# A graph network kernel on one Trainium2 core: the inverse square root of three layers' layer norms, by Newton's iteration on VectorE

## The chip, the cores and the metric

The kernel runs on one core of a Trainium2 chip. A core has a matrix engine (TensorE, in profiles PE), and three engines for the rest: VectorE (DVE), ScalarE (ACT) and GpSimd (POOL, almost unused here). A fifth, SyncE (SP), issues the transfers between the chip's memory and the on-chip memory. Each engine works through its own list of instructions in order and waits for others by semaphores, so an instruction that has to wait holds up everything behind it on its engine.

The metric is the time on the device, in microseconds (us). The kernel before takes 3764.35 us, the median of 3 runs (3759.23 to 3766.67).

## The reference

A batch of 16 graphs with 1024 nodes of 128 features passes through four layers, each a graph layer whose result is added to its input, and a layer norm over the features:

```python
def _layernorm(x, axis=-1, eps=1e-5):
    m = jnp.mean(x, axis=axis, keepdims=True)
    v = jnp.var(x, axis=axis, keepdims=True)
    return (x - m) / jnp.sqrt(v + eps)

x = _layernorm(x + L0(x, adj))   # sum over neighbours, times U, relu, over degree
x = _layernorm(x + L1(x, adj))   # masked attention: relu(q) relu(k)^T, softmax, times v
x = _layernorm(x + L2(x, adj))   # four-headed graph attention, weights from two vectors
x = _layernorm(x + L3(x, adj))   # neighbours thinned out row by row, three SAGE layers
```

Layer 1 needs q, k and v of the whole graph, and its result x2 is the input of layer 2. Layer 3 thins out the adjacency ("dilation", a sequential rule over rows) and has batch norms over all graphs between its three parts, so it can start only when all graphs are through.

## The kernel before

Nodes lie in 8 blocks of 128, one node per partition, features along the free axis. One function, `fuse`, does layers 0 to 2 and the dilation for all 16 graphs; `sage` does layer 3 after it.

In `fuse` the work is written as eleven generators, among them `layer0`, `layer1` (keys and values), `scores`, `values` (attention), `layer2` (weights and sides), `sides`, `layer2_sums`, `signs` (turns the loaded adjacency into the marks `has` and `over`), `widen` and `dilate`. Each yields a `Step` before the instructions that belong to it: the engine, a cost in us that the author estimates, and what it must follow. A planner, `Loom`, replays these costs: it always takes the step that can start first by its own reckoning, and among those of the same engine within 0.5 us the one that is due first. The due times come from a period of 160 us per graph and a phase and stretch for each generator. The instructions are written out in the order in which the planner takes the steps; the framework below it then still moves single instructions of one engine past others that don't depend on them. So a changed cost of one step can move any instruction of `fuse`.

The lines concerned:
- `Norm` is a layer norm of 8 blocks. `take` gathers statistics of a block (L547). `apply` combines them (L555 to L558 on VectorE), takes the square root on ScalarE (L560), then the reciprocal and the shift (L562 to L564 on VectorE), and applies both to the 8 blocks on ScalarE (L568). It runs three times for each graph, 48 times in all: for x1 after layer 0, for x2 after `values`, for x3 after layer 2.
- What follows x1: transposes on PE, the copy `xt` (L653), q and k (L681, L684). What follows x2: the copy `xt2` (also L653), a row of weights `t_row` (L818) that goes through memory and comes back spread (`row`, L763), and `st` (L835). What follows x3: its store to memory (L998).
- ScalarE has in the same stretches: `has` and `over` (L334, L337), `wide` (L352), the softmax `pr` (L719, an Exp), the copies `pt` (L737), the rows of the thinned adjacency `adt` (L531), the marks `sg` (L782), `ac` (L871, L872, Exp) and `bd` (L912, Exp).
- VectorE has: the running counts `up` and `ranked` (L367, L369) of the dilation, its rounds (`part`, L431 and L432; `thr`, L408 to L418; `ranked`, L494 to L505), the row minimum `low` (L716), `g` (L791, which needs `sg`), `sums` (L967) and the weights' `src` and `pieces` (L884 to L900).

[...]where the needed function is not in the table that is loaded, a table load (ACT_TABLE_LOAD in profiles) stands ahead of the instruction. The norms of layer 3 (L84, L1147 and the row norms at L1122) have square roots of their own, in `sage`.

Of the kernel before, what the change touches and what calls it, by code (L numbers as in the profile page):

```python
# [11 lines left out]
I32 = mybir.dt.int32  # L12
# [4 lines left out]
AF = mybir.ActivationFunctionType  # L17
ALU = mybir.AluOpType
PSUM = bass.MemoryType.PSUM
DRAM = bass.MemoryType.DRAM  # L20
P = 128
# [171 lines left out]
def fuse(S, ctx, a, x3, adt_d, viol, B=16):  # L193
# [18 lines left out]
    tc, nc = S.tc, S.nc  # L212
    const, ident, ones = S.scope(ctx, "fuse_const"), S.ident, S.ones
    V = nc.vector
    x_d, adj, mask = a["x"], a["adj"], a["nodemask"]
    a2 = a["L2_gnn_a"]
    H, DH = a2.shape[0], a2.shape[1] // 2
    N, TWOS, NEVER, ROUNDS = 8 * P, 2.0**24, 1e5, 2
    HI, NEG, REACH = 9e13, 9e15, 40.0
    D1, W3 = DH + 1, 3 * (DH + 1)  # L220

    two = ctx.enter_context(tc.tile_pool(name="fuse_two", bufs=2, space=PSUM))
    one = ctx.enter_context(tc.tile_pool(name="fuse_one", bufs=2, space=PSUM))
# [315 lines left out]
    class Norm:  # L539
# [8 lines left out]

        def apply(self, mark):

            yield Step("DVE", 0.4)
            t = sm.tile([P, 6, 8, 1], F32, name="ln_t")
            both, apart, var, sd, rs, nb = (t[:, i, :, :] for i in range(6))
            e, o, se, so = (self.st[:, :, i : i + 1] for i in (1, 4, 2, 5))
            V.tensor_tensor(apart, e, o, ALU.subtract)  # L555
            V.tensor_tensor(var, se, so, ALU.add)
            V.scalar_tensor_tensor(apart, apart, P / 4.0, apart, ALU.mult, ALU.mult)
            V.tensor_tensor(var, var, apart, ALU.add)  # L558
            yield Step("ACT", 1.5)
            nc.scalar.activation(sd, var, AF.Sqrt, bias=S.eps, scale=1.0 / P)  # L560
            yield Step("DVE", 0.35)
            V.tensor_tensor(both, e, o, ALU.add)  # L562
            V.reciprocal(rs, sd)
            V.scalar_tensor_tensor(nb, both, -0.5, rs, ALU.mult, ALU.mult)  # L564
            for q in range(2):
                yield Step("ACT", 1.55, mark=f"{mark} {q}")
                for c in range(4 * q, 4 * q + 4):
                    nc.scalar.activation(  # L568
                        self.y[:, c, :], self.y[:, c, :], AF.Identity, bias=nb[:, c, :], scale=rs[:, c, :]
                    )  # L570
# [667 lines left out]
def tile_gnn_stack(tc, a, out):  # L1238

    nc = tc.nc
    with ExitStack() as outer:
        flag = outer.enter_context(tc.tile_pool(name="flag", bufs=1))
        viol = flag.tile([P, 8], F32, name="viol")
        nc.vector.memset(viol, 0.0)
        with ExitStack() as ctx:
            S = Setup(ctx, tc)
            dram = ctx.enter_context(tc.tile_pool(name="fast_dram", bufs=1, space=DRAM))  # L1250
            x3 = dram.tile([16, 8 * P, P], F32, name="x3")
            adt_d = dram.tile([16, 8, P, 8 * P], F8, name="adt_d")
            with ExitStack() as first:
                fuse(S, first, a, x3, adt_d, viol)
            with ExitStack() as third:
                layers = [[a[f"L3_gnn_{n}{i}"] for n in ("Wr", "Wx", "b", "g", "be")] for i in (1, 2, 3)]
                sage(S, third, x3, a["nodemask"], adt_d, layers, a["L3_gnn_Wl"], a["L3_gnn_bl"], out)
            todo = flag.tile([1, 1], I32, name="todo")
            with tc.tile_pool(name="flag_ps", bufs=1, space=PSUM) as fp:
                ps = fp.tile([1, 8], F32, name="ps_flag")  # L1260
                nc.tensor.matmul(ps, S.ones[:, 0:1], viol, start=True, stop=True)
                total = flag.tile([1, 1], F32, name="total")
                nc.vector.tensor_reduce(total, ps, mybir.AxisListType.X, ALU.max)
                nc.vector.tensor_copy(todo, total)
        v = nc.values_load(todo[0:1, 0:1], min_val=0, max_val=16384)
        with tc.If(v > 0):
            general(tc, a, out)
# [676 lines left out]
```

## Time and profile before

| what | value |
|---|---|
| median of the runs | 3764.35 us (3759.23 to 3766.67) |
| profiled execution, its own time | 3761.21 us |
| its span, first to last instruction | 3759.5 us |
| mean granted clock of PE | 0.896 |
| PE busy | 3074.1 us (82%) |
| VectorE busy | 2937.3 us (78%), 7545 instructions |
| ScalarE busy | 2281.2 us (61%), 3889 instructions |
| table loads on ScalarE | 94, of 1283 ns each |

The profile is of one execution. A group line gives the source line, the engine and operation, what is written and read with shapes, and how often; then the busy time in all and the mean of one in ns; then the idle time of the engine just before these instructions and what ended it. A timeline line gives the start in us, the duration, the engine, the line, and in brackets the idle time before it. "The chain that ended last" follows the execution back from its end, at each step to what released it. `fuse` fills the first 2590 us or so.

### The profile page before, as it was taken

The numbers are of one execution on the slowest core, as the hardware profiler recorded it, in microseconds if no ns is written. First come the engines' busy times: TensorE is split into PE (matmuls) and PEld (weight loads), VectorE is DVE, ScalarE is ACT, GpSimd is POOL, SyncE is SP. The second block draws the span as 40 slices with busy tenths as digits, with TensorE's granted clock in tenths as the row PEclk, the third lists the DMA queues.
The fourth block names the chain that finished last, engine by engine and source line by source line (L and its number), as shares of the span: only waits on it lengthen the run. The fifth ranks groups of instructions, "written<-read, shape, count | busy, mean of one in ns | idle before, by whom it ended". The sixth has DMA issues, their size and how long they took to land.

```text
span 3759.5 us, 68072 instructions
## 1 busy us (share of the span) xinstructions
PE 3074.1 (82%) x26884; PEld 2402.0 (64%) x26884; DVE 2937.3 (78%) x7545; ACT 2281.2 (61%) x3889; POOL 2.3 (0%) x10
## 2 busy tenths in 40 slices
PE   5898878988889888898888989776699899899421
PEld 3777667776677767777667776655466666666321
DVE  3677878877888778887788777886588788888777
ACT  6678686786867868678686786753355344233100
POOL 0000000000000000000000000000000000000000
PEclk8898989999899998999989999888899999999655
DMA  4011111111111111111211111100433121112122
GB/s 118 29 61 58 53 63 39 53 59 61 63 38 54 57 63 58 39 57 55 65 58 40 57 52 63 51 29 25 95 101 90 47 68 57 57 57 73 43 73 63
DMA packets 223817, 220.11 MB, mean 59 GB/s; under 512 B 47808, under 2 KB 197824, under 8 KB 223488
## 3 DMA queue, kind: packets, MB, share of 16 engines
q1 hardware_dynamic: 223488, 215.67, 18.6%
q8 instruction: 213, 3.49, 0.4%
q14 instruction: 116, 0.95, 0.1%
HBM read 181.80 MB, written 33.82 MB: 57 GB/s over the span
## 4 chain that ended last, share of the span: by engine, by line
DVE 38%; PE 34%; ACT 18%; DMA 4%; issue 4%; SPq 1%; ACTq 0%; DVEq 0%
PE ps_s L708 6%; PE ps_g L1104 6%; DVE up L367 5%; PE ps_a L744 5%; ACT sg L782 5%; PE ps_z L1060 3%; PE ps_flip L574 3%; DVE t L1113 2%; ACT x L568 2%; DVE g L791 2%; DMA a<-in_adj_dram 2%; ACT has L334 2%; DVE ranked L369 2%; DVE both L390 2%; DVE ranked L494 1%
## 5 line engine op out<-in xcount | busy, mean ns | idle before, releaser
L782 ACT ACTIVATE sg<-row,st 128x1024 int8<-128x1024 f32 x512 | 555.6, 1141 | 7.3 <-DVE g L791 6.6
L1104 PE MATMUL ps_g<-pz,ad 128*128 128x384 bf16 (+1 forms) x3072 | 534.2, 327 | 2.2 <-DMA ad<-adt_d 2.2
L1104 PEld LDWEIGHTS <-ad 128*128 128x128 fp8e4 x3072 | 297.8, 98 | 199.8 <-DMA ad<-adt_d 12.1
L960 PE MATMUL ps_b<-pieces,g 128*128 128x198 bf16 x4096 | 372.6, 247 | 7.9 <-DVE sums L967 7.9
L960 PEld LDWEIGHTS <-g 128*128 128x128 fp8e4 x4096 | 351.8, 95 | 29.5 <-issue 28.8
L708 PE MATMUL ps_s<-kt,qt 128*128 128x512 f32 x512 | 315.5, 702 | 29.2 <-ACT pr L719 26.0
L935 PE MATMUL ps_m<-pieces,has 128*128 128x132 bf16 x3072 | 225.0, 241 | 127.5 <-ACT pieces L891 57.1
L935 PEld LDWEIGHTS <-has 128*128 128x128 fp8e4 x3072 | 218.5, 106 | 133.5 <-issue 133.4
L1121 ACT ACTIVATE sq<-xw 128x128 f32<-128x128 f32 x384 | 117.7, 307 | 306.1 <-DVE xw L1114 271.9
L744 PEld LDWEIGHTS ps_a<-vn,pt 128*128 128x128 f32 x2048 | 257.9, 199 | 61.9 <-ACT pt L737 30.5
L791 DVE TENSOR_TENSOR g<-sg,has 128x1024 int16<-128x1024 int16 x256 | 175.2, 685 | 153.0 <-ACT sg L782 151.7
L367 DVE TENSOR_TENSOR_SCAN up<-wide 128x1024 f16<-128x1024 bf16 x128 | 290.4, 2279 | 2.5 <-ACT wide L352 1.0
L744 PE MATMUL ps_a<-vn,pt 128*128 128x128 f32 x2048 | 270.5, 285 | 22.6 <-ACT pt L737 22.5
L719 ACT ACTIVATE pr<-ps_s,low 128x1024 f32<-128x1024 f32 x128 | 142.5, 1113 | 184.0 <-DVE low L716 179.8
L624 PE MATMUL ps_g<-py,has 128*128 128x128 bf16 (+1 forms) x3072 | 205.2, 224 | 34.6 <-DVE ranked L369 26.7
L716 DVE TENSOR_REDUCE low<-ps_s 128x1 f32<-128x1024 f32 x128 | 156.1, 1220 | 82.5 <-PE ps_s L712 82.4
L624 PEld LDWEIGHTS <-has 128*128 128x128 fp8e4 x3072 | 190.4, 100 | 37.8 <-DVE rdeg L631 20.9
L1113 DVE TENSOR_REDUCE t<-ps_g 128x128 f32<-128x384 f32 x384 | 206.3, 546 | 5.1 <-PE ps_g L1104 4.9
L531 ACT ACTIVATE adt<-ps_n 128x512 fp8e4<-128x512 f32 x256 | 146.2, 598 | 97.1 <-PE ps_n L521 88.8
L1060 PE MATMUL ps_z<-wzx,raw 128*128 128x256 f32 x768 | 191.9, 393 | 12.5 <-DVE xw L1068 5.6
L1224 PE MATMUL ps_y<-wl,raw 128*128 128x128 f32 x256 | 56.5, 410 | 161.7 <-DVE y L1228 161.7
L334 ACT ACTIVATE has<-a 128x1024 fp8e4<-128x1024 f32 x136 | 143.0, 1051 | 71.7 <-DMA a<-in_adj_dram 55.7
(239 smaller groups left out, 6574.2 us busy)
## 6 DMA issues: line engine op xcount, KB each, us to landing
a<-in_adj_dram SPq DMA_DIRECT2D x136, 512.0 KB
ad<-adt_d SPq DMA_DIRECT2D x384, 128.0 KB
row<-t_d SPq DMA_DIRECT2D x64, 512.0 KB
adt_d<-adt SPq DMA_DIRECT2D x128, 128.0 KB
xn<-x SPq DMA_DIRECT2D x32, 512.0 KB
x<-in_x_dram SPq DMA_DIRECT2D x16, 512.0 KB
x<-x SPq DMA_DIRECT2D x16, 512.0 KB
out_dram<-xn SPq DMA_DIRECT2D x16, 512.0 KB
```

Of the source, the lines that this page charges most:

```text
L334: nc.scalar.activation(has[c][:, r, :], t, AF.Sign, accum_out=num0[c][:, r : r + 1], saturate=False)
L367: V.tensor_tensor_scan(up, wide[k, r], wide[k, r], 0.0, ALU.add, ALU.max)
L624: nc.tensor.matmul(ps_g[:, k, 0:e], has[b][:, jb, ib * P : (ib + 1) * P], py[:, jb, q * P : q * P + e], start=(jb == 0 and q == 2), stop=( ...
L708: nc.tensor.matmul(ps_s[:, f : f + 512], qt[:, ib * P : (ib + 1) * P], kt[:, f : f + 512], start=True, stop=False,)
L744: nc.tensor.matmul(ps_a[:, 0:P], pt[:, c * P : (c + 1) * P], vn[:, c, :], start=(c == 0), stop=(c == 7))
L782: nc.scalar.activation(sg[:, k, :], rows[b, h], AF.Sign, bias=st[:, 1, h, ib : ib + 1], scale=-1.0)
L791: V.tensor_tensor(side[h, q // 2][:, q % 2 * 2 : q % 2 * 2 + 2, :].bitcast(I16), sg.bitcast(I16), has[b][:, 2 * q : 2 * q + 2, :].bitcast( ...
L935: nc.tensor.matmul(ps_m[:, u // 2, o : o + H * D1], has[b][:, ib, jb * P : (jb + 1) * P], pieces[:, ib, 1, :, t, :], start=(t == 0 and ib ...
L960: nc.tensor.matmul(ps_b[:, u // 2, (u % 2) * 2 * W3 : (u % 2 + 1) * 2 * W3], side[h, q][:, k, jb * P : (jb + 1) * P], pieces[:, 4 * q + k, ...
L1060: nc.tensor.matmul(ps_z[:, k, :], raw[:, b, c * P : (c + 1) * P], wzx, start=True, stop=True)
L1104: nc.tensor.matmul(ps_g[:, 0:width], adt[jb][:, ib * P : (ib + 1) * P], pz[:, jb, 0:width], start=(jb == 0), stop=(jb == 7),)
L1113: nc.vector.tensor_reduce(t, ps_g[:, 0 : 3 * P].rearrange("p (t d) -> p d t", t=3), AX.X, ALU.add)
```

## The change

The four instructions that combine the statistics stay. The square root on ScalarE and the reciprocal on VectorE go. In their place VectorE scales the variance and adds the epsilon, makes a first guess of 1/sqrt by arithmetic on the bits of the float read as an integer (minus half of them plus a constant), and improves it by three rounds of Newton's iteration, three instructions each. That makes one VectorE step of eleven more instructions less the reciprocal. The three steps (VectorE 0.4, ScalarE 1.5, VectorE 0.35) are one step of 1.6 on VectorE for the planner. All other steps and their costs, the 1.6 of `ac` among them, are as before.

```diff
-    D1, W3 = DH + 1, 3 * (DH + 1)
+    D1, W3, GUESS = DH + 1, 3 * (DH + 1), float(0x5F3759DF)
...
         def apply(self, mark):
 
-            yield Step("DVE", 0.4)
+            yield Step("DVE", 1.6)
             t = sm.tile([P, 6, 8, 1], F32, name="ln_t")
-            both, apart, var, sd, rs, nb = (t[:, i, :, :] for i in range(6))
+            both, apart, var, y, z, nb = (t[:, i, :, :] for i in range(6))
             e, o, se, so = (self.st[:, :, i : i + 1] for i in (1, 4, 2, 5))
             V.tensor_tensor(apart, e, o, ALU.subtract)
             V.tensor_tensor(var, se, so, ALU.add)
             V.scalar_tensor_tensor(apart, apart, P / 4.0, apart, ALU.mult, ALU.mult)
             V.tensor_tensor(var, var, apart, ALU.add)
-            yield Step("ACT", 1.5)
-            nc.scalar.activation(sd, var, AF.Sqrt, bias=S.eps, scale=1.0 / P)
-            yield Step("DVE", 0.35)
+            V.tensor_scalar(var, var, 1.0 / P, 1e-5, ALU.mult, ALU.add)
+
+            V.tensor_scalar(y.bitcast(I32), var.bitcast(I32), -0.5, GUESS, ALU.mult, ALU.add)
+            for _ in range(3):
+                V.tensor_tensor(z, y, y, ALU.mult)
+                V.scalar_tensor_tensor(z, z, -0.5, var, ALU.mult, ALU.mult)
+                V.scalar_tensor_tensor(y, z, 1.5, y, ALU.add, ALU.mult)
             V.tensor_tensor(both, e, o, ALU.add)
-            V.reciprocal(rs, sd)
-            V.scalar_tensor_tensor(nb, both, -0.5, rs, ALU.mult, ALU.mult)
+            V.scalar_tensor_tensor(nb, both, -0.5, y, ALU.mult, ALU.mult)
+            rs = y
             for q in range(2):
                 yield Step("ACT", 1.55, mark=f"{mark} {q}")
```

From L558 on, line numbers of the changed kernel are up to four higher: what was L568 is L572 there, and L567 is the last VectorE instruction of the norm (L564 before).

## The prediction

> **What bounds the kernel now.** I read the page first: busy times and the chain that ended last.
>
> ```profile
> PE 3074.1 (82%) x26884; PEld 2402.0 (64%) x26884; DVE 2937.3 (78%) x7545; ACT 2281.2 (61%) x3889; POOL 2.3 (0%) x10
> ...
> DVE 38%; PE 34%; ACT 18%; DMA 4%; issue 4%; SPq 1%; ACTq 0%; DVEq 0%
> ```
>
> No engine is full, and the chain hops between three. So a microsecond saved on ScalarE (ACT) is worth something only where ScalarE paces. Next, the groups of ScalarE that the norms cause:
>
> ```profile
> L560 ACT ACT_TABLE_LOAD x47 | 60.3, 1283 | 0.8
> ...
> L719 ACT ACT_TABLE_LOAD x29 | 37.2, 1283 | 0.5
> ...
> L871 ACT ACT_TABLE_LOAD x16 | 20.5, 1283 | 0.3
> ...
> L560 ACT ACTIVATE ln_t<-ln_t,eps 128x8 f32<-128x8 f32 x48 | 14.4, 300 | 121.1 <-DVE ln_t L558 120.7
> ```
>
> Each square root brings a table load, and the next Exp (L719, L871) brings another. Where do they lie? The page's slices show layers 0 to 2 until about 2590 us; between the x2 norms of two batches the chain repeats every 157.05 us (1070.16 to 1227.21). I cut one such period, from 1227.2, into 16 windows; the columns are window, length, busy us (instructions) of PE, weight loads, DVE, ACT and POOL, granted clock, DMA share, GB/s:
>
> ```profile
> 1237.01:1246.83 9.81, 9.63 (x119) 8.29 (x117) 1.32 (x4) 6.88 (x12) 0.00 (x0) 1.00 0.47 162
> 1246.83:1256.64 9.81, 7.57 (x125) 7.16 (x123) 8.64 (x14) 9.26 (x13) 0.00 (x0) 1.00 0.08 28
> 1256.64:1266.45 9.81, 2.48 (x35) 2.02 (x33) 9.81 (x23) 8.12 (x10) 0.00 (x0) 0.74 0.10 40
> ...
> 1305.70:1315.51 9.81, 9.81 (x83) 8.13 (x82) 6.83 (x12) 9.34 (x15) 0.00 (x0) 1.00 0.48 159
> 1315.51:1325.33 9.81, 6.54 (x68) 3.46 (x67) 8.80 (x26) 7.94 (x13) 0.00 (x0) 0.70 0.40 130
> 1325.33:1335.14 9.81, 7.45 (x51) 5.40 (x49) 6.86 (x29) 8.57 (x15) 0.00 (x0) 0.50 0.11 41
> ...
> 1374.39:1384.20 9.81, 9.20 (x97) 6.76 (x95) 9.29 (x33) 0.81 (x3) 0.00 (x0) 1.00 0.18 53
> ```
>
> From 1256.6 to 1276.3 VectorE (DVE) is 100% busy, and near the x2 norm (last row) 95%; in the second row it shares the load with ScalarE. From 1305.7 to 1335.1, the start of a batch's attention, ScalarE is busy 9.34 + 7.94 + 8.57 = 25.9 of 29.4 us, while PE has holes and its clock falls to 0.50: there ScalarE paces. The timeline of that stretch:
>
> ```profile
> 1317.79 1.28 ACT L719 ACT_TABLE_LOAD   x1
> 1319.08 1.11 ACT L719 ACTIVATE pr<-ps_s,low 128x1024 f32<-128x1024 f32 x1
> ...
> 1325.97 1.28 ACT L560 ACT_TABLE_LOAD   x1
> 1327.27 0.30 ACT L560 ACTIVATE ln_t<-ln_t,eps 128x8 f32<-128x8 f32 x1
> ...
> 1333.92 1.28 ACT L719 ACT_TABLE_LOAD   x1
> ```
>
> Three table loads and a root stand in it (those of the x3 norm). The first is on the chain itself (one period earlier, at 1160.68).
>
> **What the Trainium skill says.** "ScalarE: Activation LUTs", section "Table sets: the hidden batching unit": exp and sqrt are in different sets, so alternating them loads every time. The trace agrees: 47 loads at the root, 46 at an Exp. The same page, "What ACT_TABLE_LOAD costs", gives 1283 ns plus a drain of 1380 ns. The trace shows the 1283 ns, but pr starts at 1319.08, 0.01 us after the load ended at 1319.07: no drain, so I use 1.283 us. "VectorE: DVE Perf Modes", section "The DRAIN you can't avoid": a read of what the instruction before wrote needs a semaphore. The built program has such a wait on each dependent link. "TensorE: Matmul & The Clock Gate", section "What's actually happening": PE falls to half clock after an idle window of about 3.4 us. The windows agree (0.50, 0.70).
>
> **The change part by part.** All is per steady batch unless said.
>
> *Removed table loads.* In the built program's order 94 loads stand ahead of the end before, and two after (the first Sign; layer 3's first root). 92 × 1.283 = 118.0 us, and 48 roots of 0.30 = 14.4: ScalarE loses 132.4 us, 8.3 per batch. What is it worth?
> - In 1305.7 to 1335.1: 3 × 1.28 + 0.3 less the 0.09 that neighbours overlap = 4.1 us. At least the 1.28 on the chain counts. Not all: `has` waits for the adjacency load twice here (1.11 and 1.21 us), and these waits grow when the rest gets quicker; the release-to-landing time is about 3.5 us (over ends 1312.86, has starts 1316.14). I take 3.0, bounds 1.3 and 4.1.
> - The x1 root (1279.02): ScalarE's L568 started 0.1 us after it was free, but VectorE was full and gave the L564 it needs no earlier (1126.00 one period before, so 1283.05; L568 started at 1283.28). Worth 0; covered by VectorE, and 1.6 if that cover were gone.
> - The x2 root: L568 waited 2.19 us for VectorE's L564; worth 0. Without that cover it would be 1.6.
> - L871's load (1254.79) lies before VectorE's full stretch, hidden by scans; 0, bound 1.3.
>
> *Added VectorE work.* Per norm, eleven instructions come and one (reciprocal, 195 ns) goes: +10, in all +480. None is in the trace, but the same shapes are (128x8, 160 to 167 ns). Independent ones start 0.08 us apart (61.72, 61.81, 61.90), a dependent one 0.19 us after its source (L557 61.98, L558 62.17). The new chain has 13 dependent links. In the new order a steady cycle spans two batches, six norms; between the first and last instruction of each stand 18, 14, 18, 1, 17 and 15 other VectorE instructions. So five norms are interleaved and cost 10 × 0.08 = 0.8 us; the sixth, an x2, is exposed: 4 × 0.08 + 13 × 0.19 = 2.8, less the 0.6 that its seven old ones took interleaved, about 2.0 to 2.2. By place: x1 (VectorE full) +0.8; x2 (95% full) mean of 0.8 and 2.0, +1.4; x3 (VectorE at 70 to 90%, something idle) +0.3, bounds 0 and 0.8. Sum +2.5. Behind the later L572 (old L568) on ScalarE's queue stand adt, the copy xt2 and with them t_row; these prices include their delay.
>
> *Moved instructions.* The planner orders by its own costs (a VectorE step of 1.6 now, no ScalarE step of 1.5), so everything moves. I looked for what matters. Before, after x2's apply, ScalarE runs three `sg` before the first `wide`, and VectorE's first `g` stands ahead of `ranked`: it waits 5.98 us for sg (at 1245.79) with scans behind it. This is the hole in the first window row (DVE 1.32 of 9.81). In the new order no sg stands before the wides, and the first g comes after five or more scans. 3 × 1.04 = 3.1 us less stands before wide; adt's waits for PE remain, so I take 2.0 (0 to 3.1). The queue of SP: the eight loads of an adjacency now all stand ahead of the x3 store, before six did; the last two were released at 1342 anyway. Worth 0.
>
> *Sum.* −3.0 − 2.0 + 2.5 = −2.5 per batch. About 14 batch periods are steady: −35 us. Layer 3's first root now loads its table: +1.3, hidden or not. 3761.2 (the profiled execution) − 34 = 3727; the median of the runs lies 3.1 above that execution, so about **3731**.
>
> **The rivals.**
> *Slower: VectorE sets the pace.* Place: 1256.6 to 1276.3 and 1374.4 to 1384.2. If the moved wides gain nothing and the attention start gives only its 1.3, then with x3 at 0.8 the batch gets −1.3 + 0.8 + 1.4 + 0.8 = +1.7; 14 × 1.7 = 24, about 3789. The two-batch cycle speaks for it: from one x2 norm to the next the new order has 361 and 307 VectorE entries in turn (a run of one instruction counted once), where before it was 303 each time. If the heavy batch is paced by VectorE, its 27 above the mean, at 127 us / 334 = 0.38, are 10 us, of which the light one may return only half: 5 per pair, 2.5 a batch, 35 in all, 3799. It decides once ScalarE's relief in the attention start and the wides' gain together fall below the 2.5 that VectorE pays. Against: DVE is only at 70 to 90% there.
> *No change.* The relief turns into waits of L572 for L567 and of `has` for the load: ScalarE idles more by what it saved. The gain of 2.5 is met by 2.5: 3764.
> *The change doesn't do it* (another function still needs a second table): excluded, the built order has the two loads only.
>
> **How the numbers follow.** This kernel can be told from no change at about 0.2%, 7.5 us. Faster, near 3731: 0.53. No change: 0.09. Slower, 3789 to 3799: 0.38, high because a replanned order can lose several us per batch in places I didn't cost. Range: best per batch −4.1 − 3.1 + 2.2 = −5 gives 3694; above, the VectorE rival at 3789 with little more: 3692 to 3800. The likeliest case alone: 3700 to 3752.
>
> **What would show it.** Two table loads; ScalarE near 2149 us busy, VectorE up by about 40 to 50; no 6 us wait of g for sg after x2; the stretch from the first has to the second pt about 3 us shorter, PE's clock there above 0.5; the pair of batches near 309 us instead of 314. Wrong if L572's waits for L567 pass 5 us a batch, if `has` waits for loads grow by 2 us or more, or if the pair takes over 314.

## The result, and the profile after

The changed kernel takes **3857.45 us** (median of 4 runs, 3851.76 to 3866.49). The kernel before, run beside it, takes 3763.93 us. The ratio is 1.0252 (95% interval 1.0239 to 1.0265): the change costs about 94 us, 2.5%. The forecast was 3731, and 3800 was the end of its range.

The first part of the page after, and its chain that ended last:

```profile
PE 3102.7 (81%) x26868; PEld 2431.7 (63%) x26884; DVE 2993.8 (78%) x8025; ACT 2157.8 (56%) x3749; POOL 2.3 (0%) x10
...
PE 41%; DVE 39%; ACT 11%; DMA 5%; issue 2%; SPq 1%; ACTq 0%; DVEq 0%
```

The sizes of the parts came close to the forecast: ScalarE lost 123.4 us of busy time (132.4 were expected), VectorE gained 56.5 us (40 to 50) and 480 instructions. ScalarE's share of the chain fell from 18% to 11%, but PE's rose from 34% to 41%. ScalarE's groups of table loads in all:

```profile
L334 ACT ACT_TABLE_LOAD x1 | 1.3, 1283 | 0.8 <-PEq L1934 0.8
L1126 ACT ACT_TABLE_LOAD x1 | 1.3, 1283 | 0.0
```

The 92 loads are gone; the change did what it says. So the time went elsewhere. The last scaling of a norm starts at 2673.6 us (L572), against 2585.4 before (L568): `fuse` ends 88 us later. In the steady part the order repeats every two batches, and two batches are one window here, first of the kernel before, then of the changed one (window, length, busy us and instructions of PE, weight loads, VectorE, ScalarE, GpSimd; granted clock, DMA share, GB/s):

```profile
1227.20:1541.30 314.10, 272.57 (x2712) 221.69 (x2711) 253.66 (x625) 239.36 (x348) 0.00 (x0) 0.92 0.17 55
```

```profile
1449.20:1777.00 327.80, 275.56 (x2719) 223.66 (x2720) 261.81 (x687) 223.37 (x331) 0.00 (x0) 0.89 0.16 53
```

The pair takes 13.7 us more. ScalarE does 16.0 us less in it. VectorE does 8.2 us more and idles 5.6 us more as well (327.80 - 261.81 = 66.0 against 314.10 - 253.66 = 60.4). Over the whole kernel the span grows by 90.3 us; 56.5 of that is VectorE's busy time and 33.8 its idle time (span less busy time). Where is the idle time? The list of waits (who waited for whom: us in total, times, longest), before:

```profile
DVE g L791 <- ACT sg L782: 151.7, 91, 6.0
...
DVE ranked L369 <- PE ps_n L521: 37.1, 15, 9.9
```

and after:

```profile
DVE ranked L369 <- PE ps_n L521: 176.6, 15, 14.7
...
PE ps_flip L578 <- ACT x L572: 107.2, 17, 12.1
...
DVE g L795 <- ACT sg L786: 84.8, 58, 4.6
```

The wait of `g` for `sg` shrank by 67 us, as the prediction said. In its place `ranked` waits 140 us longer for PE. `ranked` has one buffer. PE's `stays` (L515 to L521) read the thinned rows of one dilation out of it, and the next dilation can't write its first row before they are done. But these 140 us are not all new. VectorE's timeline in the kernel before, from the last drop of one dilation (L505) to the first row of the next (start, duration, line; in brackets the idle time before):

```profile
1229.23 0.67 DVE L505 TENSOR_TENSOR ranked<-x,y 128x1024 bf16<-128x1024 bf16 x1
...
1230.03 4.46 DVE L367 TENSOR_TENSOR_SCAN up<-wide 128x1024 f16<-128x1024 bf16 x2
...
1239.11 0.23 DVE L835 COPY st<-ps_st 128x64 f32<-128x64 f32 x1 [3.59 <-PE ps_st L828]
...
1245.79 0.69 DVE L791 TENSOR_TENSOR g<-sg,has 128x1024 int16<-128x1024 int16 x1 [5.98 <-ACT sg L782]
1247.82 1.29 DVE L369 TENSOR_TENSOR ranked<-up,wide 128x1024 f16<-128x1024 f16 x2 [1.34 <-PE ps_n L521]
```

`st`, `g` and `ranked` share one hole here, and `ranked` closes it: no third scan stands in it, since `wide` has two buffers and `ranked` gives them back. The same stretch in the changed kernel, around an x2 norm:

```profile
1584.32 2.28 DVE L367 TENSOR_TENSOR_SCAN up<-wide 128x1024 f16<-128x1024 bf16 x1
1586.52 0.66 DVE L505 TENSOR_TENSOR ranked<-x,y 128x1024 bf16<-128x1024 bf16 x1
...
1587.44 2.28 DVE L367 TENSOR_TENSOR_SCAN up<-wide 128x1024 f16<-128x1024 bf16 x1
...
1589.94 0.17 DVE L555 TENSOR_TENSOR ln_t<-ln_st 128x8 f32<-128x8 f32 x1
...
1592.81 0.17 DVE L567 SCALAR_TENSOR_TENSOR ln_t<-ln_t 128x8 f32<-128x8 f32 x1
...
1608.51 1.29 DVE L369 TENSOR_TENSOR ranked<-up,wide 128x1024 f16<-128x1024 f16 x2 [14.42 <-PE ps_n L521]
```

and PE's, in the same stretch:

```profile
1593.56 0.33 PE L578 MATMUL ps_flip<-ident,x 128*128 128x128 f32 x1 [2.85 <-ACT x L572]
```

Two scans of the next dilation stand ahead of the x2 norm; the norm (3.0 us, its links 0.20 us apart) runs after the last drop (L505); PE's transposes of x2 wait for its scaling, and the rest of the stays stands behind them on PE's queue. Then VectorE idles 14.42 us, in one wait where there were three. Before, the norm began 7.5 us ahead of the end of the last drop in every steady batch, so it ran among the drops. After, it begins 7.6 us ahead in one batch and 2.8 us behind in the next.

The late norm does hold up the stays, but the sum changes little. From the end of the last drop to the first row of the next dilation it is 17.9 us in a steady batch before, and about 21.3 (norm behind) and 16.3 us (norm ahead) in turn after: 0.9 more in the mean. VectorE's idle time in these 15 stretches, added up from the timelines, is 170.9 us before and 182.1 after. So only 11 of the 34 us of added idle time lie in this hole. `ranked` waits for 9.1 us there even where the norm is ahead; most of the 140 us have only changed their name.

### The profile page after: what moved, and what is told of

Its sections match the earlier page's. It is cut to its first block, busy times and chain, and to the rows that moved or that the text cites. A ratio compares the mean times of both kernels' runs of the same rounds, so it can differ in the third digit from the quotient of the medians.

```text
span 3849.8 us, 68421 instructions
## 1 busy us (share of the span) xinstructions
PE 3102.7 (81%) x26868; PEld 2431.7 (63%) x26884; DVE 2993.8 (78%) x8025; ACT 2157.8 (56%) x3749; POOL 2.3 (0%) x10
## 4 chain that ended last, share of the span: by engine, by line
PE 41%; DVE 39%; ACT 11%; DMA 5%; issue 2%; SPq 1%; ACTq 0%; DVEq 0%
PE ps_g L1108 7%; DVE up L367 5%; PE ps_s L712 5%; PE ps_a L748 4%; PE ps_m L939 4%; PE ps_z L1064 3%; ACT sg L786 3%; PE ps_b L964 3%; PE ps_flip L578 3%; PE ps_g L628 2%; DMA a<-in_adj_dram 2%; DVE t L1117 2%; DVE both L461 2%; DVE g L795 2%; ACT has L334 1%
## 5 line engine op out<-in xcount | busy, mean ns | idle before, releaser
L964 PEld LDWEIGHTS <-g 128*128 128x128 fp8e4 x4096 | 350.0, 96 | 21.3 <-issue 20.5
L939 PEld LDWEIGHTS <-has 128*128 128x128 fp8e4 x3072 | 220.3, 107 | 100.2 <-issue 98.9
L723 ACT ACTIVATE pr<-ps_s,low 128x1024 f32<-128x1024 f32 x128 | 142.0, 1109 | 219.5 <-DVE low L720 166.6
L748 PE MATMUL ps_a<-vn,pt 128*128 128x128 f32 x2048 | 261.0, 280 | 1.8 <-ACT pt L741 1.4
L795 DVE TENSOR_TENSOR g<-sg,has 128x1024 int16<-128x1024 int16 x256 | 175.1, 687 | 96.3 <-ACT sg L786 84.8
L628 PE MATMUL ps_g<-py,has 128*128 128x128 bf16 (+1 forms) x3072 | 240.6, 234 | 9.9 <-ACT has L334 5.6
L628 PEld LDWEIGHTS <-has 128*128 128x128 fp8e4 x3072 | 214.7, 106 | 16.6 <-ACT has L334 6.2
L369 DVE TENSOR_TENSOR ranked<-up,wide 128x1024 f16<-128x1024 f16 x128 | 85.9, 682 | 176.6 <-PE ps_n L521 176.6
L741 ACT COPY pt<-ps_flip 128x1024 f32<-128x1024 f32 x128 | 129.0, 1009 | 105.7 <-PE ps_flip L578 104.3
```

The lines of the kernel that those rows point to most:

```text
L628: nc.tensor.matmul(ps_g[:, k, 0:e], has[b][:, jb, ib * P : (ib + 1) * P], py[:, jb, q * P : q * P + e], start=(jb == 0 and q == 2), stop=( ...
L748: nc.tensor.matmul(ps_a[:, 0:P], pt[:, c * P : (c + 1) * P], vn[:, c, :], start=(c == 0), stop=(c == 7))
L795: V.tensor_tensor(side[h, q // 2][:, q % 2 * 2 : q % 2 * 2 + 2, :].bitcast(I16), sg.bitcast(I16), has[b][:, 2 * q : 2 * q + 2, :].bitcast( ...
L939: nc.tensor.matmul(ps_m[:, u // 2, o : o + H * D1], has[b][:, ib, jb * P : (jb + 1) * P], pieces[:, ib, 1, :, t, :], start=(t == 0 and ib ...
L964: nc.tensor.matmul(ps_b[:, u // 2, (u % 2) * 2 * W3 : (u % 2 + 1) * 2 * W3], side[h, q][:, k, jb * P : (jb + 1) * P], pieces[:, 4 * q + k, ...
```

## The experiments

Two theories stood first. **Work**: VectorE's added instructions cost the time, in any order. **Order**: the planner's new order costs it, whatever the arithmetic. All times are medians, beside the kernel before on the same chip (3759 to 3765 us).

### The two halves, each alone

The first kernel has Newton's iteration with the old planned steps, so that the order is nearly that of before:

```diff
-            yield Step("DVE", 1.6)
+            yield Step("DVE", 0.4)
...
+            yield Step("ACT", 1.5)
+            yield Step("DVE", 0.35)
             V.tensor_scalar(var, var, 1.0 / P, 1e-5, ALU.mult, ALU.add)
```

> Newton's iteration as in the changed kernel, but the planner is told the old three steps (VectorE 0.4, ScalarE 1.5, VectorE 0.35), so the order of all other work is nearly that of before. Theory 'order' (the 94 us come from the order that the planner made of the new costs): the arithmetic alone gives what the prediction's first two steps gave, -3.0 + 2.5 = -0.5 a batch, so 3740 to 3775, and the pair of batches takes about 313 us. Theory 'work' (VectorE's 50 us more are the cause in any order): 3820 to 3860, the pair about 325.

Measured: 3810.52 us, ratio 1.0126 (1.0109 to 1.0143), so +46 us, between the two expectations.

The second has the old arithmetic with the new planned step (one of 1.6 on VectorE, with the root inside it):

```diff
-            yield Step("DVE", 0.4)
+            yield Step("DVE", 1.6)
...
-            yield Step("ACT", 1.5)
             nc.scalar.activation(sd, var, AF.Sqrt, bias=S.eps, scale=1.0 / P)
-            yield Step("DVE", 0.35)
```

> The arithmetic of before (the root on ScalarE, 94 table loads back), with the changed kernel's planner costs (one VectorE step of 1.6 that also holds the root), so the order is nearly that of after. Theory 'order': as slow as the changed kernel or slower, 3850 to 3900, the pair 328 to 332 us. Theory 'work': near before, 3755 to 3785, the pair about 314.

Measured: 3812.99 us, ratio 1.0134 (1.0117 to 1.0151), so +49 us. Neither theory alone holds: the halves are 46 and 49, and together (95) they make the whole 94. The wait of `ranked` for `ps_n` is 157.9 us in the second kernel and 83.6 in the first, so it comes mostly with the order. But the loop through `ranked` is not what makes the second kernel slow: from the last drop to the next first row it takes about 18.2 and 14 us in turn, less than the 17.9 before, and still the kernel is 49 us slower. (VectorE also waits 10.2 us there for the root inside its step, 6.7 more than before, which the order's 49 include; and this order brings 80 table loads, not 94.)

### The price of the loads, and of the iteration

The third kernel leaves the square root out, so its norms divide by the variance plus epsilon; the table loads go with it, and the planned order stays:

```diff
-            nc.scalar.activation(sd, var, AF.Sqrt, bias=S.eps, scale=1.0 / P)
+            nc.scalar.activation(sd, var, AF.Identity, bias=S.eps, scale=1.0 / P)
```

> The order and steps of before, with Identity in place of Sqrt: the square root of the norms of layers 0 to 2 is left out (they divide by the variance plus epsilon), and with it the table loads. It prices the removal of the loads alone, the prediction's first step: -3.0 a batch (1.3 to 4.1) would be 3707 to 3746, about 3722. If the relief turns into other waits (theory 'hidden'): 3755 to 3765. Theories 'order' and 'work' both allow either.

Measured: 3752.15 us, ratio 0.9966 (0.9952 to 0.9979): the loads were worth 12 us, 0.75 a batch, under the prediction's lowest bound of 1.3 and a little more than "hidden" has. Newton in the old order therefore costs 3810.5 - 3752.2 = 58 us, 3.6 a batch. Where did the rest of the relief go? ScalarE's timeline at the start of a batch's attention, in the kernel before:

```profile
1319.08 1.11 ACT L719 ACTIVATE pr<-ps_s,low 128x1024 f32<-128x1024 f32 x1
...
1335.22 1.11 ACT L719 ACTIVATE pr<-ps_s,low 128x1024 f32<-128x1024 f32 x1
...
1338.45 1.11 ACT L719 ACTIVATE pr<-ps_s,low 128x1024 f32<-128x1024 f32 x1 [1.52 <-DVE low L716]
```

and without the root:

```profile
1312.34 1.11 ACT L719 ACTIVATE pr<-ps_s,low 128x1024 f32<-128x1024 f32 x1
...
1324.64 1.10 ACT L719 ACTIVATE pr<-ps_s,low 128x1024 f32<-128x1024 f32 x1
...
1332.42 1.11 ACT L719 ACTIVATE pr<-ps_s,low 128x1024 f32<-128x1024 f32 x1 [6.07 <-DVE low L716]
```

The second softmax row comes 12.3 us after the first instead of 16.1, but the third comes 20.1 after it instead of 19.4: the relief has turned into a wait of 6.07 us. It is the same over the whole kernel: ScalarE's waits of `pr` for `low` grew from 179.8 to 252.0 us and those of L560 for L558 from 120.7 to 166.6, together by 118 us, as much as the loads took. Behind the third row's wait is PE, which runs at a granted clock of 0.56 there before and 0.58 without the root (windows from the first to the third row). PE's first transposes of the attention wait for VectorE's count in both kernels, in the kernel before and then without the root:

```profile
1327.84 1.94 PE L574 MATMUL ps_flip<-ident,pr 128*128 128x128 f32 x8 [1.03 <-DVE gone L452]
```

```profile
1321.47 1.94 PE L574 MATMUL ps_flip<-ident,pr 128*128 128x128 f32 x8 [1.03 <-DVE gone L452]
```

From the first `pt` to the row minimum of the third row it is 7.3 us before (1329.81 to 1337.14) and 7.4 without the root (1323.74 to 1331.10): that is mostly PE's matmuls at half clock (the eight transposes above take 1.94 us, and 1.07 at 1339.01, at full clock). The Trainium skill, "TensorE: Matmul & The Clock Gate", section "What's actually happening", has PE fall to half clock after an idle window of about 3.4 us. The traces agree in kind, over stretches a little shorter than that: the granted clock falls from 1.00 to 0.50 after 2.9 us in which PE worked 0.6 us (before), and after 2.6 us with 0.2 us of work (without the root). ScalarE was the busiest engine there, and yet not the one that set the pace.

The fourth kernel has six rounds of the iteration for three, in the old order:

```diff
-            for _ in range(3):
+            for _ in range(6):
```

> As the first kernel (Newton, old steps), with six rounds of the iteration for three: nine more VectorE instructions a norm, 27 a batch. Theory 'order': what VectorE's small instructions cost is 0.08 us each where other work is interleaved and 0.19 each where not, so 0.7 to 1.7 us a norm and 2.2 to 5.1 a batch at most, half of it hidden: 15 to 50 us above the first kernel. Theory 'work': VectorE paces, so at least the 50 us that the first three rounds cost again and more, 70 to 100 us above the first kernel.

Measured: 3902.86 us, ratio 1.0379 (1.0362 to 1.0396), 92 us above three rounds. That is 92.3 / (48 x 9) = 0.214 us for each added instruction, a little over the 0.20 us between dependent links, though "half of it" hidden was expected under the order theory. That it is so near the 0.20 is partly chance: VectorE's busy time grew by 44 us and its idle time by 45, and its wait of `st` for PE, which follows the x2 norm by way of the scaling and the transposes, from 104.6 to 166.4.

The fifth, again with the old steps, runs the iteration on GpSimd, which does nothing else:

```diff
+            G = nc.gpsimd
...
             for _ in range(3):
-                V.tensor_tensor(z, y, y, ALU.mult)
-                V.scalar_tensor_tensor(z, z, -0.5, var, ALU.mult, ALU.mult)
-                V.scalar_tensor_tensor(y, z, 1.5, y, ALU.add, ALU.mult)
+                G.tensor_tensor(z, y, y, ALU.mult)
+                G.tensor_tensor(z, z, var, ALU.mult)
+                G.tensor_scalar(z, z, -0.5, 1.5, ALU.mult, ALU.add)
+                G.tensor_tensor(y, y, z, ALU.mult)
+            yield Step("DVE", 0.35)
             V.tensor_tensor(both, e, o, ALU.add)
             V.scalar_tensor_tensor(nb, both, -0.5, y, ALU.mult, ALU.mult)
```

> Old steps and order; the iteration runs on GpSimd, which is idle otherwise (14 small instructions a norm there, since it takes a round in four), so VectorE loses the reciprocal and gains nothing, and the table loads stay away. Theory 'occupancy' (what Newton cost in the old order, 58 us above the version without root, is VectorE's time): 3740 to 3765. Theory 'latency' (it is the length of the chain that the norm's scaling waits for): longer than on VectorE, since GpSimd takes at least as long for each link: 3810 or above, to 3880.

Measured: 3862.20 us, ratio 1.0255 (1.0238 to 1.0272). The result falls to the latency theory by its number, but the list of waits shows that it doesn't separate the two:

```profile
DVE ln_t L570 <- POOL ln_t L567: 114.7, 45, 4.0
```

The last instruction of the norm stayed on VectorE, and VectorE stood still for it 114.7 us: a chain of some 3.9 us did not fit into the room that the order leaves. Against the kernel without root this one is 110 us slower. Leaving out the waits for something else behind them, the instructions of the 48 norms hold VectorE for 34 us without the root, 78 with Newton and 134 with six rounds (from the starts in the timeline): 44 more for 58 us of run time, then 56 more for 92. Beside that, VectorE's idle time from the last drop to the next first row, which the x2 norm leads up to, grows from 168 to 193 and 225 us. In the GpSimd kernel the hold stays at 34 us, and the 114.7 us of waiting come back as 110. So both count in the old order: the time that a norm takes of VectorE, and the waiting behind a norm that ends later. These runs don't part the two any further.

### Is it the two-batch order?

The prediction's rival had uneven batches as its ground. Three kernels keep the changed text and differ only in the planned cost, 1.3 here, 0.75 and 0.4 in the others:

```diff
-            yield Step("DVE", 1.6)
+            yield Step("DVE", 1.3)
```

> The changed kernel with a planned cost of 1.3 for the norm's one VectorE step in place of 1.6; all else is the same text. In the built order every batch has the same number of VectorE instructions (325 between two x2 norms; in the changed kernel 363 and 286 in turn). Theory 'two-batch' (the order's 49 us come from uneven batches): near the kernel with Newton and the old steps, 3795 to 3820, one batch near 160.5 us. Theory 'one step' (any order that sees the norm as one VectorE step, with no room for ScalarE in it, loses): 3845 to 3870.

> The same with a planned cost of 0.75, the sum of the two VectorE steps of before; 321 VectorE instructions in every batch. Theory 'two-batch': 3790 to 3820. Theory 'one step': 3845 to 3870.

> The same with a planned cost of 0.4. Here the built order alternates again, with 302 and 343 VectorE instructions in turn, about half the unevenness of the changed kernel (286 and 363). Theory 'two-batch': between the even orders and the changed kernel, 3820 to 3850. Theory 'one step': 3845 to 3870. If it lies with the even ones, the count of instructions by batch is not what matters.

Measured: 3873.17 (1.0282; 1.0265 to 1.0299), 3863.09 (1.0263; 1.0246 to 1.0280) and 3844.12 us (1.0211; 1.0194 to 1.0228). The last lies where "two-batch" had it, but the two even orders are no faster than the changed kernel, and an uneven one is: unevenness isn't the cause. For the "one step" theory, a kernel with three steps again, the empty one told as 2.0. Against the changed kernel:

```diff
-            yield Step("DVE", 1.6)
+            yield Step("DVE", 0.4)
...
                 V.scalar_tensor_tensor(y, z, 1.5, y, ALU.add, ALU.mult)
+            yield Step("ACT", 2.0)
+            yield Step("DVE", 0.35)
             V.tensor_tensor(both, e, o, ALU.add)
```

This edit differs in two things from the Newton kernel with the old steps, not in one as the expectation has it: the empty step is 2.0 and not 1.5, and the iteration stands ahead of it, in the first step, where that kernel has it in the third.

> Newton with three planned steps as before, only that the empty ScalarE step is told as 2.0 in place of 1.5; every batch has 324 VectorE instructions. Theory 'three steps' (an order that leaves room between the norm's steps keeps the old time): 3800 to 3820, as with 1.5. Theory 'tuned point' (the old costs happen to give a good order, and any other planned cost loses some 1%): 3830 to 3875.

Measured: 3894.04 us, ratio 1.0349 (1.0332 to 1.0367), 84 us above the kernel with 1.5. So three steps alone don't make an order fast, and the "one step" theory doesn't hold as it was put; which of the two differences costs the 84 us was not tested. It is the third theory, "tuned point", that stands here by its direction; its range ended at 3875.

### Taking away the wait for the buffer

The rows of `ranked` come from ten buffers for eight, so that two rows of the next dilation needn't wait for PE; for the room, `xt0` shares the buffers of `d` and `y`:

```diff
-        ranked[c] = p1.tile([P, 8, N], F16, name="ranked")
+        ranked[c] = [p1.tile([P, N], F16, name="ranked", bufs=10) for _ in range(8)]
...
-                xt = p2.tile([P, 4, P], F32, name="xt0")
+                xt = p4.tile([P, 4, P], F32, name="xt0", tag="t2k", bufs=2)
```

It was tried on the changed kernel, on the kernel before, and on Newton with the old steps.

> The changed kernel, with the eight rows of ranked (the tile that the next dilation must get back from PE's stays) taken from ten row buffers in place of eight, so that two rows of the next dilation can be written before PE has read the last drop; for the room, xt0 shares the buffers of d and y. Theory 'dilation loop' (what the new order lost is the 12 us wait of ranked L369 for PE's ps_n, 176.6 us against 37.1 before): two scans and two ranked rows, 5.8 us, run in each of 15 waits, so the wait falls to about 90 and the time by 50 to 85 us, to 3770 to 3810. Theory 'symptom' (VectorE is behind for another reason and would only wait elsewhere): 3845 to 3860, the wait moves to row 2 or to another line.

> The kernel before with the same ten row buffers. Its wait of ranked for ps_n is 37.1 us in all. Theory 'dilation loop': all of it can go, 3730 to 3750. Theory 'symptom': 3758 to 3768.

> Newton with the old steps (3810.5 measured) and ten row buffers; its wait of ranked for ps_n is 83.6 us. Theory 'dilation loop': 5.8 us in each of 15 waits at most, 3735 to 3770. Theory 'symptom': 3800 to 3812.

Measured: 3779.55 us (1.0038; 1.0026 to 1.0051), **3728.39 us** (0.9905; 0.9888 to 0.9921) and 3763.48 us (0.9996; 0.9987 to 1.0005). They gain 78, 36 and 47 us. The second is faster than both kernels of this case, 1.0% faster than the one before. In all three, two rows of the next dilation are now written ahead of the wait, and VectorE idles less from the last drop to the first row that has to wait: by 86, 62 and 76 us. In the changed kernel the wait fell from 176.6 to

```profile
DVE ranked L369 <- PE ps_n L521: 92.6, 15, 9.2
```

as the "dilation loop" theory has it. In the third it did not fall (83.6 and 84.9 us); the wait of `st` for PE went there, from 104.6 to 0.9. The loop through this buffer is thus a limit of all three kernels, the one before too, and only what is left of the difference tells of the change: with ten rows it costs 51 us (3779.6 against 3728.4), with eight 94. With ten rows the two orders with Newton differ by 16 us only (3779.6 and 3763.5), against 47 with eight. The edit also gives every row a buffer of its own and moves `xt0`; a kernel with eight such rows, which would part these from the two added rows, was not run.

Does that hold without Newton, and does the loop also hide ScalarE's relief? Two kernels with ten rows tell: the one without root (the square root is left out again), and the old arithmetic in the changed order. Their edits are those above, combined.

> The order of before, ten row buffers for ranked, and Identity for Sqrt: the square root of these norms is left out, and with it the table loads. Against the kernel before with ten row buffers (3728.4). Theory 'hidden by the loop' (the ranked buffer's loop hid ScalarE's relief): the relief grows to 25 us or more, 3690 to 3703. Theory 'ScalarE is not the limit anywhere for long': 8 to 16 us as with eight rows, 3712 to 3720.

> The root and table loads of before in the changed kernel's order, with ten row buffers. With eight it took 3813.0, 49 us more than before, and its wait of ranked for ps_n was 157.9 us. Theory 'all in that wait': 5.8 us in each of 15 waits come back, 3725 to 3745, as fast as the kernel before with ten rows. Theory 'half of it': 3750 to 3775, as the pair with Newton (3763.5 in the old order, 3779.6 in the new) showed 16 us left.

Measured: 3707.59 us (0.9859; 0.9839 to 0.9878) and 3816.18 us (1.0146; 1.0129 to 1.0163). The relief is worth 3728.4 - 3707.6 = 21 us with ten rows, or 15 if each kernel is set against the kernel before on its own chip, and 12 with eight: the loop did not hide most of it, and whether it hid any is within the noise. The time lies between the two expectations. The other is a miss: the old arithmetic in the changed order gains nothing from ten rows. Its waits with eight rows, and with ten:

```profile
DVE ranked L369 <- PE ps_n L521: 157.9, 15, 13.2
DVE g L789 <- ACT sg L780: 89.7, 86, 3.3
```

```profile
DVE g L789 <- ACT sg L780: 175.6, 122, 4.8
...
DVE ranked L369 <- PE ps_n L521: 65.8, 15, 7.4
```

92 us went from the one wait and 86 came back in the other: with the roots still on ScalarE, its marks `sg` are late next. So the parts don't simply add. With eight rows Newton costs 44 us in this order (3813.0 to 3857.5); with ten rows it gains about 40 (3816.2 to 3779.6, on two chips that differ by 6 us in the kernel before).

### What makes an order slow?

The planner knows of other rings of buffers, but not of `ranked`. A kernel told it:

```diff
-            yield Step("DVE", 0.61, give=[("wide", (k, r))])
+            yield Step("DVE", 0.61, take=[] if r else [("ranked", k)], give=[("wide", (k, r))])
...
-            yield Step("PE", 0.7, after=() if i else (f"drop {k} 7",), take=[("dps", 0)], mark=f"stays {k} {i}")
+            yield Step("PE", 0.7, after=() if i else (f"drop {k} 7",), take=[("dps", 0)], mark=f"stays {k} {i}", give=[("ranked", k)] if i == 15 else [])
...
-    loom = Loom(160.0, two=2, one=2, dps=2, wide=2, g=4, pr=2, a=2)
+    loom = Loom(160.0, two=2, one=2, dps=2, wide=2, g=4, pr=2, a=2, ranked=1)
```

> The changed kernel, with the planner told that the first ranked row of a dilation takes a buffer which the last stays of the dilation before gives back; eight rows as in the changed kernel. It orders everything anew, 322 to 325 VectorE instructions in every batch. Theory 'the planner's not knowing is the loss': other work is put ahead of ranked, its wait for ps_n falls below 80 us, and the time to 3790 to 3825. Theory 'tuned point' (any new order loses): 3840 to 3890, whatever that wait is.

Measured: 3819.24 us, ratio 1.0153 (1.0136 to 1.0170). The time falls as hoped, but the wait doesn't:

```profile
DVE ranked L369 <- PE ps_n L521: 211.3, 15, 15.3
```

So the total of this wait doesn't rank the orders, although two more rows help the changed one. The last three kernels move phases alone:

```diff
-        (loads(batches), 80.0, 2.2), (widen(batches), 108.0, 1.0), (dilate(batches), 107.0, 1.0),
+        (loads(batches), 80.0, 2.2), (widen(batches), 108.0, 1.0), (dilate(batches), 113.0, 1.0),
```

That is the first, on the changed kernel. The second, on the changed kernel too, has 109 there and 145 for the 148 of `values`. The third, on the kernel before, has 105.

> The changed kernel with the phase of dilate at 113 in place of 107; in the built order the x2 norm stands 8 VectorE instructions ahead of the last drop (L505) in every batch (in the changed kernel 18 ahead and 16 behind in turn; before, 16 ahead). Theory 'position' (an x2 norm behind the last drop holds up PE's stays, and so the next dilation): near the Newton kernel with the old steps, 3795 to 3825. Theory 'tuned point' (any moved order loses, whatever the position): 3845 to 3895.

> The changed kernel with the phases of values and dilate at 145 and 109 (148 and 107); the x2 norm stands 43 VectorE instructions ahead of the last drop in every batch. Theory 'position': 3780 to 3825. Theory 'tuned point': 3845 to 3895.

> The kernel before, root and table loads and all, with the phase of dilate at 105 in place of 107; the x2 norm stands 16 VectorE instructions behind the last drop in every batch. Theory 'position': as much slower as the changed kernel's order or more, since it is in every batch and not in every second: 3810 to 3860. Theory 'no matter': 3755 to 3785.

Measured: 3862.15 (1.0263; 1.0245 to 1.0280), 3917.90 (1.0412; 1.0394 to 1.0429) and 3841.86 us (1.0214; 1.0197 to 1.0231). The counts in these expectations run to the last drop but one, and the second of them has another norm for that of x2. By the trace, measured to the end of the last drop, x2's norm begins 4.9 us ahead in the steady batches of the first, and 2.8 us behind in most batches of the second. The third is the clean one. There is no Newton in it, every instruction is one of the kernel before, and two microseconds of one phase cost 79 us; x2's norm begins 5.9 us behind the end of the last drop in the steady batches. That is what "position" asked for. But the first of the three, with the norm ahead, is slow as well (its wait of `ranked` for `ps_n` is only 39.7 us), and the told order, with the norm 2.8 us behind in every batch, is the fastest of the moved ones. Position isn't the whole rule.

All orders with the changed kernel's arithmetic and eight rows, by time: old steps 3810.5; told of the buffer 3819.2; planned 0.4: 3844.1; planned 1.6, the change: 3857.5; phase 113: 3862.2; planned 0.75: 3863.1; planned 1.3: 3873.2; three steps with 2.0: 3894.0; phases 145 and 109: 3917.9. With the old arithmetic: before 3763.9, changed order 3813.0, phase 105 3841.9. These ran on several chips, whose kernels before differ by up to 6 us. Every moved order is slower than the one that was kept, by 9 to 107 us. The change's own order, at 47, is an ordinary one of them.

**What stays open** is which property of an order sets its time. Neither the evenness of the batches, nor the total wait for `ps_n`, nor the place of x2's norm ranks them. Nor does VectorE's idle time between the last drop and the next first row: it is 220.5 us in the told order, the fastest of the moved ones, and 170.6 with the phase at 113, which is 43 us slower.

## Why the prediction was wrong

- *Removed table loads*, "I take 3.0, bounds 1.3 and 4.1": 0.75 a batch. This step failed. It took ScalarE for the pace-setter of the attention's start since it was the busiest; PE at half clock and VectorE's count set the pace, and ScalarE's relief went into waits for them. The stretch from the first softmax row to the second `pt` did not get 3 us shorter: 21.04 us before (1319.08 to 1340.12), 21.19 without the root (1312.34 to 1333.53), and PE's clock rose by 0.02 only. The 1.283 us of a load was right. (The 3.5 us from release to landing are 3.28 by the two times given.)
- *Added VectorE work*, +2.5: the mechanism was right, and the size of VectorE's share nearly so. Without the waits behind them, the 48 norms hold VectorE for 34.5 us before, 78.3 with Newton in the old order and 82.6 in the changed kernel, 2.7 and 3.0 a batch more. But the price in run time was 3.6 a batch in the old order, against the kernel without the root: the term left out the waiting that a longer x2 norm causes behind it. The links stood 0.20 us apart.
- *Moved instructions*, "I take 2.0": this is the step that failed most, and in sign. The stalls of `g` did shrink, from 151.7 to 84.8 us, but no more than two scans fit ahead of `ranked`, and the hole stayed (170.9 us before, 182.1 after), under the name of `ranked`. I took the wait of `g` for the end of the hole. Its next one already stood in the profile of before, 1.34 us of `ranked` for PE's stays right behind `g`, and part of the hole in the window row was the wait of `st`. So the 2.0 a batch were not there to be won. That the order then lost 2.9 a batch (46.9 / 16) is measured; where it loses them is open, since only 11 us of the added idle time lie in this hole.
- The sum for the whole kernel: -12 (loads) + 58 (Newton, old order) + 47 (from there to the changed kernel) = 93, so the last term is what is left over; the old arithmetic in the changed order measured it apart, at 49. The forecast had -35.
- *The rival "VectorE sets the pace"* was right about the arithmetic, at 46 us where it had 24 to 35. Its ground, uneven batches, was wrong: even orders are as slow. Its place was not shown: VectorE is busy for 56.5 us more and idle for 33.8 more, and the traces don't tie either to its full stretch. It left out the order as a cost of its own, though "can lose several us per batch in places I didn't cost" stood in the text.
- *No change* and *the change doesn't do it* are out: the loads are gone, and the time isn't the same.
- *What would show it*: two loads, ScalarE near 2158 and VectorE up by 56 (not 40 to 50) came about as said. Of the three signs of error one appeared: the pair took 327.8. L572's waits for L567 are 33.8 us in all, 22.3 of them once at the end (under the 5 a batch named), and the waits of `has` for loads did not grow (55.7 and 55.3 us). The signs named were for the places I had costed.
- *The range* should have held a term for a replanned order. Nothing in the profile of before gives its size; the test that shows it most plainly, a phase moved by 2 us with nothing else changed, cost 79 us.

## What to carry to other kernels

Where a planner with due times writes the order, a changed cost is a second change: price the arithmetic in the kept order, and put the new order beside it as a term of its own; here every other order was slower by 9 to 107 us, and keeping the old planned costs would have saved half of the loss. Before a stall is counted as gain, look at the instruction behind it: if that one was released just afterwards, as `ranked` was 1.34 us behind `g`, the stall only changes its name, and the longest wait in a list need not be what the change cost. An engine's busy share in a stretch doesn't make it the pace-setter: follow the wait of the next instruction (here the third softmax row) back before a saving is counted. And where a single buffer closes a loop over two engines, two more rows of it are cheap to try: they gave 36 us to the kernel before, while the change still loses in the same buffers (3779.6 against 3728.4, and 3763.5 with the old planned costs).

## What the runs showed of the hardware

- Small dependent instructions (128x8) on VectorE follow each other 0.20 us apart, and independent ones 0.08 us. With six rounds instead of three each added one came back as 0.214 us of run time, half of it busy time of VectorE and half idle time. I had expected other work between them to hide more.
- On GpSimd the same instructions (128x8) take about 0.20 us each and start 0.28 us apart when dependent (1375.01, 1375.29, 1375.57), so a link there is only 1.4 times as long as on VectorE; a round takes four of them there and three on VectorE.
